# A decoder layer on one core: the end of the FFN in seven tiles of 128 tokens instead of eight of 112, and new tables of the order

## The chip, the cores and the metric

The kernel runs on one core of one Trainium2 chip. The metric is the device time of one execution in microseconds (us); smaller is better. In the profile the core's engines are called PE (TensorE, matmuls), PEld (its weight loads), DVE (VectorE), ACT (ScalarE), POOL (GpSimd) and SP (SyncE, which only issues transfers). Each engine works through its own queue in order and waits there for what its next instruction needs.

## What is computed

One layer of a decoder with post-norm, for 8 sequences of 112 tokens with 256 channels (896 tokens), all in float32:

```python
x = layernorm(x + self_attention(x))               # 16 heads of 64
x = layernorm(x + cross_attention(x, ctx, mask))   # 16 heads of 16, 375 keys
x = layernorm(x + ffn(x))

def ffn(x_):                                       # x_: (896, 256)
    idx = argmax(x_ @ router.T)                    # one of 8 experts a token
    y = down[idx] @ (silu(gate[idx] @ x_) * (up[idx] @ x_))        # hidden 512
    ys = (silu(x_ @ w_gate_s.T) * (x_ @ w_up_s.T)) @ w_down_s.T    # shared expert
    return y + ys

def layernorm(x):                                  # no scale, no shift of its own
    return (x - mean(x)) / sqrt(var(x) + 1e-5)
```

## The kernel before

**The order of the work** is written out by hand. Nine steps run one after another (lines 562 to 578 and 899). In step s three sequences are at work: the self-attention of sequence s, the cross-attention of sequence s-1, and what is left of sequence s-2. A step is a table of words (lines 28 to 50); `step` (line 532) reads the words from left to right and calls the piece of each, and since every engine's queue is in order, a table fixes how the pieces stand on every engine. `STEP` serves steps 1 to 5; `FIRST`, `STEP6`, `STEP7` and `LAST` serve steps 0, 6, 7 and 8. A `+` at a word has VectorE copy the piece's result out of the matmul memory (PSUM), a `-` has ScalarE do it.

The words of the steps:

- `k`, `u`, `c`: projections that are prepared ahead (queries and keys of the next pair of sequences, values, keys and values of the context). A product of them goes through the helper at line 248.
- `s`, `e`, `w`, `t`, `v`: scores, exponentials, weights, transposes and attention of self-attention (lines 329 to 379); `o`, `n`: its output projection and norm (381, 390); `q1`, `q2`: transposes and queries for the cross-attention (404, 408).
- `S`, `E`, `W`, `U`, `T`, `V`: the same of cross-attention (431 to 503), four heads at a time. `S` writes two score buffers, and the ring has two (line 86); `s` writes one.
- `F1` to `F4`: output projection, norm, transposes and router product of sequence s-2 (508 to 528); `f1` to `f4` are those of the last sequence.

**The FFN** is in `LAST`. `a0` to `a3` and `b0` to `b3` are the shared expert's gate and up products for the first half of the tokens (`shared_raw`, 607, of 448 = 4 x 112 tokens), `h0` to `h3` both products for the second half (`shared_half`, 615), `g0` and `g1` the silu of the first half (`silu_raw`, 627). `r` and `p` (`route_1`, 686) choose each token's expert; `R` and `P` (`route_2`, 700) count its place, `place_i`, and POOL scatters the tokens' rows to these places in DRAM (`to_places`, 661, one indirect DMA a sequence). `L` loads each expert's 128 rows (864), `A` transposes them, `B` makes the gate and up products, `C` the down product, which is stored to DRAM as `y_d` (796 to 831). A ninth, small tile takes up to 32 rows beyond an expert's 128; `x` (`beyond`, 739) works out whose they are. `C0` to `C4` also load the weights of experts 4 to 7 and of the small tile (880).

Then comes the end, once for each sequence b: `Y` gathers the 112 rows of the sequence from `y_d` by `place_i` (676), `D` adds the shared expert's down product, takes mean and variance and raises the variance to the power -0.5 on POOL (632, 224), and `Z` normalizes on VectorE and stores (643):

```python
def normalize(dst, src, mean, rs):
    V.tensor_scalar(dst, src, mean, rs, ALU.subtract, ALU.mult)
```

The store goes out on SP. A last branch (920) repeats part of this where more rows are left; with these inputs it isn't taken.

Of the kernel before, what the change touches and what calls it, by code (L numbers as in the profile page):

```python
# [25 lines left out]


STEP = """
S0 E0 k2 s0 u1- e0 T00+ F1 w0 c0 T02- S1 E1 u0- T01+ t00+ W0 s1 T10- T11- e1 c1 T12+ U0+ w1 V0 S2 c4
k3- t01- F2 F3 k0 t10+ t11- E2 v0+ v1- S3 T20+ E3 T22- o W1 T30- c2 n F4 T31+ k1- q1 U1- c3 T21+ q2  # L30
T32- V1
"""
STEP6 = """
S0 E0 c0 s0 c1 e0 T00+ T02- S1 c4 E1 w0 W0 T01- s1 u1- T10- T11- e1 u0+ U0- w1 t00- F1 T12- c3 t01-
S2 t10+ t11- V0 E2 v0+ v1- S3 T20- E3 F2 o n T21- W1 T30- c2 F3 T32- q1 F4 T22- T31- q2 U1+ V1
"""
STEP7 = """
S0 E0 c0 s0 c1 e0 S1 T00- E1 T01+ s1 c4 T02- T10- W0 U0- e1 w0 T12- w1 T11- S2 V0 t00+ t01- E2 F1
t10- v0- t11+ F2 S3 T20- v1+ E3 F3 o T30- n W1 T22- c3 T32- T21+ F4 q1 c2 T31- U1- q2 V1
"""  # L40
FIRST = """
k6 k4 u0- k5- k7+ s0 e0 s1 k3- u3- k1- e1 k2 u1- k0 w0 w1 t00+ t01+ u2- t10+ t11- v0+ v1+ z o c0 n
c1 c3 q1 c4 q2 c2
"""
LAST = """
S0 E0 F1 a2- S1 E1 a1- T00+ b0- T02+ F2 W0 T01- S2 T10+ T12- b1- E2 T11+ U0+ S3 V0 F3 E3 T20+ a3+
T22+ T21+ a0+ W1 T30- T31- F4 T32- U1- r V1 f1 R f2 b2+ f3 f4 b3- p P L0 h2 L1 h0 h1 A0 g1 A1 B0 L2
B1 A2 x C0 B2 A3 A4 C1 C2 B3 B4 A5 A6 C3 B5 C4 B6 A7 C5 B7 g0 A8 C6 B8 C7 C8 Y0 Y1 Y2 Y3 D0 Y4 Y5 D1
h3 Z0 Y6 D2 Z1 Y7 D3 Z2 D4 Z3 D5 Z4 D6 Z5 D7 Z6 Z7
"""  # L50


# [1 line left out]
def decoder_layer(  # L54
# [19 lines left out]
    E, _, H = upT.shape  # L74
    KH = H // P
    NTT = NT // P
    HB = B // 2
    HT = HB * S

    NG = 4  # L80
    NOV = (NT - 1) // P
# [2 lines left out]
    const = ctx.enter_context(tc.tile_pool(name="const", bufs=1))  # L84
# [4 lines left out]
    V, A, G = nc.vector, nc.scalar, nc.gpsimd  # L89
# [7 lines left out]
    def m_tile():  # L97
        return ps_m.tile([P, 512], F32, tag="mm", name="mm")
# [10 lines left out]
    ac = sa.enter_context(tc.tile_pool(name="ac", bufs=1))  # L109
# [5 lines left out]
    wo1 = ac.tile([P, NC, D], F32, name="wo1")  # L115
    bo1 = ac.tile([S, D], F32, name="bo1")
    xres = const.tile([S, B, D], F32, name="xres")
    r = const.tile([S, B, D], F32, name="r")
    mv = const.tile([S, B, 2], F32, name="mv")
    x2T = const.tile([P, KD, NT], F32, name="x2T")  # L120
    lgs = const.tile([S, B, E], F32, name="lgs")
    rt = const.tile([P, KD, E], F32, name="rt")
# [1 line left out]
    load = nc.sync.dma_start  # L124
# [77 lines left out]

    xs_d = tc.dram_tile([E * NT, D], F32, name="xs_d")
    y_d = tc.dram_tile([E * NT, D], F32, name="y_d")
    fill_sb = const.tile([P, D], F32, name="fill_sb")
    G.memset(fill_sb, 0.0)

    cap = xc.tile([S, S2], F32, name="cap")
# [9 lines left out]
    def stats(dst, src):  # L218
        st = small.tile([P, 6], F32, tag="st", name="st")
        n = src.shape[0]  # L220
        V.bn_stats(st[:n], src)
        V.bn_aggr(dst, st[:n])

    def rstd_of(var):

        n = var.shape[0]
        rs = small.tile([P, 1], F32, tag="rs", name="rs")
        V.tensor_scalar(rs[:n], var, EPS, None, ALU.add)  # L228
        G.tensor_tensor(rs[:n], rs[:n], mhalf[:n], ALU.pow)  # L229
        return rs[:n]  # L230

    def normalize(dst, src, mean, rs):
        V.tensor_scalar(dst, src, mean, rs, ALU.subtract, ALU.mult)
# [8 lines left out]
    def copy(on, dst, src):  # L242

        (V.tensor_copy if on == "+" else A.copy)(dst, src)  # L244

    def product(out_, pairs):
        for i, (lhsT, rhs) in enumerate(pairs):
            nc.tensor.matmul(out_, lhsT, rhs, start=(i == 0), stop=(i == len(pairs) - 1))  # L248
# [7 lines left out]
    def project(p, half):  # L256

        if half == 0:
            qk[p] = [ap_.tile([P, NC, 2 * S], F32, tag=n, name=n) for n in ("qT", "kT")]

        def piece(on, n, c):
            ps = m_tile()
            for i in range(2):
                product(
                    ps[:, bass.ts(i, 2 * S)],
                    [
                        (wqkv[n][:, k, bass.ts(c + i, P)], xT_sb[:, k, bass.ts(p, 2 * S)])
                        for k in range(KD)
                    ],
                )  # L270
# [52 lines left out]
    class SelfAttention:  # L323
# [57 lines left out]
        def project(self, on):  # L381
            b = self.b
            G.tensor_tensor(xres[:, b, :], xres[:, b, :], bo1, ALU.add)
            ps = m_tile()
            product(ps[:S, :D], [(self.aoT[:, c, :], wo1[:, c, :]) for c in range(NC)])
            V.tensor_tensor(r[:, b, :], ps[:S, :D], xres[:, b, :], ALU.add)
            stats(mv[:, b, :], r[:, b, :])
            self.rs = rstd_of(mv[:, b, 1:2])

        def norm(self, on):  # L390
            b = self.b
            normalize(xres[:, b, :], r[:, b, :], mv[:, b, 0:1], self.rs)


    class CrossAttention:
# [112 lines left out]
        def finish_1(self):  # L508
            b = self.b
            ps = m_tile()  # L510
            product(ps[:S, :D], [(self.xoT[:, k, :], wx["o"][:, k, :]) for k in range(KD)])
            V.tensor_tensor(r[:, b, :], ps[:S, :D], xres[:, b, :], ALU.add)
            stats(mv[:, b, :], r[:, b, :])
            self.rs = rstd_of(mv[:, b, 1:2])

        def finish_2(self):
            b = self.b
            normalize(xres[:, b, :], r[:, b, :], mv[:, b, 0:1], self.rs)

        def finish_3(self):  # L520
            transposed(x2T[:, :, bass.ts(self.b, S)], xres[:, self.b, :])
# [60 lines left out]
    fc = ctx.enter_context(tc.tile_pool(name="fc", bufs=1))  # L582
# [12 lines left out]
    swd = fc.tile([P, KH, D], F32, name="swd")  # L595
# [19 lines left out]
    def shared_half(hc):
        ug = sc_tile()
        for i, w in enumerate((swu, swg)):
            product(
                ug[:, i, :HT], [(w[:, k, bass.ts(hc, P)], x2T[:, k, HT:]) for k in range(KD)]
            )  # L620
        sg = fp.tile([P, 512], F32, tag="sg", name="sg", bufs=3)
        A.activation(sg[:, :HT], ug[:, 1, :HT], AF.Silu)
        V.tensor_tensor(hS1[:, hc, :], ug[:, 0, :HT], sg[:, :HT], ALU.mult)

    rstds = {}

# [2 lines left out]
        A.activation(raw["g"][:, h, :], raw["g"][:, h, :], AF.Silu)  # L629
        V.tensor_tensor(raw["u"][:, h, :], raw["u"][:, h, :], raw["g"][:, h, :], ALU.mult)  # L630

    def last_sum(b):

        h = raw["u"] if b < HB else hS1
        ps = m_tile()
        product(
            ps[:S, :D], [(h[:, hc, bass.ts(b % HB, S)], swd[:, hc, :]) for hc in range(KH)]
        )
        V.tensor_tensor(r[:, b, :], ps[:S, :D], r[:, b, :], ALU.add)
# [18 lines left out]
    place_i = small_tile("place_i", None, I32)  # L658
# [14 lines left out]
            tc.declare_no_dep(i.ins, other.ins, reason="distinct places")  # L673
        sent.append(i)

    def from_places(b):
        G.indirect_dma_start(  # L677
            out=r[:, b, :],
            out_offset=None,
            in_=y_d[:, :],  # L680
            in_offset=bass.IndirectOffsetOnAxis(ap=place_i[:, b : b + 1], axis=0),
            bounds_check=E * NT - 1,
            oob_is_err=False,
        )
# [293 lines left out]
```

## Time and profile before

| | |
|---|---|
| median of 4 runs | 417.94 us (417.71 to 418.68) |
| the profiled execution's own time | 417.9 us |
| its span, from the first to the last instruction | 416.1 us |
| mean granted TensorE clock | 0.995 of full speed |
| step 3, from S0 to S0 of step 4 | 139.4 to 177.6 us |
| LAST, from S0 | 300.65 us |
| A0, the first expert's transposes | 340.49 us |
| the last matmul of C8 | ends at 389.46 us |
| the last norm | ends at 410.46 us |

The profile is one execution. A page of it has the busy time of each engine; a timeline has one row for each stretch of equal instructions: start and duration in us, engine, line, operation, output<-inputs, shapes, the number of instructions, and in brackets the idle time ahead of them with what ended it. Matmuls are pipelined and their ends are modelled, so a block's cost on TensorE is read from its start to the next block's start. In the rows of line 248, `mm<-xT_sb,wq` is a `k` piece, `mm<-wv,xT_sb` a `u`, `mm<-cT,wxk` and `mm<-wxv,cT` a `c`; L437 is `S`, L336 is `s`, L485 is `T`, L365 is `t`, L372 is `v`, L496 is `V`, L474 is `U`, L239 the transposes in `q1`, `F3` and `f3`.

### The profile page before, as it was taken

Reading aid. Unit: us, or ns where it says so; the run is one execution under the profiler, and the core shown is the slowest. Engines: PE = TensorE matmul, PEld = TensorE weight load, DVE = VectorE, ACT = ScalarE, POOL = GpSimd, SP = SyncE. Lnnn points to the kernel's source line nnn. Section 1 sums busy time; section 2 is a strip of 40 time slices with the busy share of each in tenths; the row PEclk is TensorE's granted clock in tenths of the full one; section 3 lists DMA queues with packets and bytes.
Section 4 is the critical chain, followed back from the end, with each engine's and each line's share of the span. In section 5 each row is a group of like instructions: output and inputs, shape, how many; then the busy total and the mean of one; then the engine's idle time right before and its main releaser. Section 6 shows DMA issues by size and latency. Waiting matters only on the chain.

```text
span 416.1 us, 8496 instructions
## 1 busy us (share of the span) xinstructions
PE 398.7 (96%) x3347; PEld 310.8 (75%) x3347; DVE 239.9 (58%) x672; ACT 187.6 (45%) x476; POOL 75.2 (18%) x111
## 2 busy tenths in 40 slices
PE   5999999999999999999999999999999989999991
PEld 4977768867886887688678877867857559999661
DVE  0173685578458666855784587489487524223173
ACT  1232465456627554654566286577476221112000
POOL 3021112103012200221030112104100520000281
PEclk9999999999999999999999999999999999999998
DMA  8980398099010001000000100000694140895132
GB/s 271 308 229 0 100 372 277 12 372 351 11 39 2 2 1 38 2 2 16 23 2 2 38 0 2 2 2 2 217 373 170 45 137 11 287 375 178 40 110 61
DMA packets 38334, 46.61 MB, mean 112 GB/s; under 512 B 2181, under 2 KB 31378, under 8 KB 38290
## 3 DMA queue, kind: packets, MB, share of 16 engines
q1 hardware_dynamic: 36978, 43.66, 32.3%
q0 software_dynamic: 768, 1.84, 1.5%
q8 instruction: 28, 0.46, 0.4%
q10 hardware_dynamic: 544, 0.52, 0.4%
q14 instruction: 16, 0.13, 0.1%
HBM read 28.41 MB, written 17.60 MB: 111 GB/s over the span
## 4 chain that ended last, share of the span: by engine, by line
PE 87%; POOL 4%; issue 4%; DMA 3%; DVE 2%; ACT 0%; SPq 0%; POOLq 0%; DVEq 0%
PE mm L248 46%; PE pt L485 10%; PE sc L248 7%; PE sc L437 7%; PE mm L496 5%; PE sc L336 4%; PE mm L372 3%; PE pt L365 3%; POOL r L677 1%; POOL xs_d L664 1%; DMA wq<-in_w_qkv 1%; POOL rs L229 1%; PE pt L239 1%; DMA xs_d<-xres,place_i 1%; DMA xs<-xs_d 1%
## 5 line engine op out<-in xcount | busy, mean ns | idle before, releaser
L455 ACT ACTIVATE ex<-ex,nm 112x375 f32<-112x375 f32 x128 | 76.5, 599 | 47.4 <-DVE nm L451 46.7
L451 DVE CUSTOM_DVE_ANT_0 ex<-sc,cap 112x375 f32<-112x375 f32 x128 | 63.6, 544 | 10.0 <-PE sc L437 9.6
L485 PEld LDWEIGHTS pt<-ident,ex 112*125 112x125 f32 x384 | 50.9, 188 | 17.1 <-issue 10.0
L485 PE MATMUL pt<-ident,ex 112*125 112x112 f32 x384 | 55.1, 275 | 0.1
L244 ACT COPY exT<-pt 125x448 f32<-125x448 f32 x56 | 28.3, 527 | 29.2 <-PE pt L485 29.1
L358 POOL TENSOR_TENSOR pr<-pr,den 112x896 f32<-112x896 f32 x16 | 26.9, 1683 | 80.3 <-DVE den L357 43.6
L229 POOL TENSOR_TENSOR rs<-rs,mhalf 112x1 f32<-112x1 f32 x24 | 13.4, 559 | 144.6 <-DVE rs L228 144.5
L248 PE MATMUL mm<-xT_sb,wq 128*128 128x224 f32 x128 | 28.9, 373 | 5.0 <-DMA wq<-in_w_qkv 5.0
L248 PE MATMUL mm<-wv,xT_sb 128*112 128x512 f32 x64 | 31.1, 608 | 0.0
L248 PEld LDWEIGHTS mm<-xT_sb,wq 128*128 128x128 f32 x128 | 24.4, 199 | 8.5 <-DMA wq<-in_w_qkv 5.0
L437 PE MATMUL sc<-kc,qz 32*112 32x375 f32 x256 | 29.8, 519 | 0.1
L248 PE MATMUL mm<-wo,aoT 128*112 128x256 f32 x128 | 29.0, 380 | 0.0
L244 DVE COPY exT<-pt 125x448 f32<-125x448 f32 x40 | 24.8, 622 | 7.0 <-PE pt L485 6.5
L248 PE MATMUL mm<-xT_sb,wk 128*128 128x224 f32 x128 | 27.4, 359 | 0.0
L248 PE MATMUL mm<-wxv,cT 128*125 128x256 f32 x96 | 25.6, 389 | 0.0
L248 PEld LDWEIGHTS mm<-xT_sb,wk 128*128 128x128 f32 x128 | 24.4, 195 | 1.5 <-issue 0.5
L248 PEld LDWEIGHTS mm<-wo,aoT 128*112 128x112 f32 x128 | 22.0, 177 | 4.5 <-DVE aoT L244 0.2
L455 ACT ACTIVATION_READ_ACCUMULATOR ex<-ex,nm 112x1 f32 x128 | 23.9, 187 | 0.0
L248 PE MATMUL mm<-cT,wxk 128*128 128x375 f32 x64 | 23.2, 486 | 0.0
L244 DVE COPY prT<-pt 112x448 f32<-112x448 f32 x16 | 9.8, 620 | 20.7 <-PE pt L365 20.7
L496 PE MATMUL mm<-exT,vc 125*32 125x112 f32 x768 | 21.7, 261 | 0.0
L345 DVE TENSOR_REDUCE mx<-sc 112x8 f32<-112x896 f32 x16 | 17.4, 1087 | 5.9 <-PE sc L336 5.4
(156 smaller groups left out, 640.4 us busy)
## 6 DMA issues: line engine op xcount, KB each, us to landing
xs_d<-fill_sb SPq DMA_DIRECT2D x1, 7168.0 KB, 24.2
y_d<-fill_sb SPq DMA_DIRECT2D x1, 7168.0 KB, 24.9
wg<-in_gateT SPq DMA_DIRECT2D x9, 512.0 KB, 7.3
wu<-in_upT SPq DMA_DIRECT2D x9, 512.0 KB, 8.0
wd<-in_downT SPq DMA_DIRECT2D x9, 512.0 KB, 9.3
cT<-in_ctxT SPq DMA_DIRECT2D x8, 375.0 KB, 3.6
wv<-in_w_qkv SPq DMA_DIRECT2D x2, 512.0 KB, 7.7
wo<-in_w_out SPq DMA_DIRECT2D x1, 1024.0 KB, 13.9
```

The costliest lines, as they stand in the source:

```text
L229: G.tensor_tensor(rs[:n], rs[:n], mhalf[:n], ALU.pow)
L244: (V.tensor_copy if on == "+" else A.copy)(dst, src)
L248: nc.tensor.matmul(out_, lhsT, rhs, start=(i == 0), stop=(i == len(pairs) - 1))
L336: nc.tensor.matmul(sc[:S, j, bass.ts(c, S)], qT[rows, 4 * g + c, self.tok], kT[rows, 4 * g + c, self.tok], start=True, stop=True,)
L345: V.tensor_reduce(self.mx, scv, AX.X, ALU.max)
L358: G.tensor_tensor(pr, pr, den.unsqueeze(3).to_broadcast([S, 2, 4, S]), ALU.mult)
L365: nc.tensor.transpose(pt[:S, bass.ts(c, S)], self.pr[g][:, j, c, :], ident[:S, :S])
L437: nc.tensor.matmul(sc[i // 2][:S, i % 2, :S2], self.qz[rows, par, c, :], kc[rows, c, :], start=True, stop=True,)
L451: V.tensor_tensor_reduce(ex[:, i, :], self.sc[g][i // 2][:S, i % 2, :S2], cap, -1.0, BIG, ALU.add, ALU.min, nm[:, i : i + 1],)
L455: A.activation(ex[:, i, :], ex[:, i, :], AF.Exp, bias=nm[:, i : i + 1], scale=-1.0, accum_out=den[:, i, g % 2 : g % 2 + 1],)
L485: nc.tensor.transpose(pt[:JT, bass.ts(i, S)], self.ex[g][:, i, bass.ts(t, JT)], ident[:S, :S])
L496: nc.tensor.matmul(av[32 * i : 32 * i + 32, 0:S], vcs[self.b % 2][:, t, 4 * c + i, bass.ds(32 * par, 32)], self.exT[2 * c + par][:, t, bas ...
```

## The change

The end works on seven tiles of 128 tokens (7 x 128 = 896) instead of eight of 112. For this the first half of the shared expert's hidden values takes 512 tokens and the second 384; `r` and `mv` get 128 partitions; and the places, which lie as [112 tokens, 8 sequences], are laid anew as [128 tokens, 7 tiles]: `i0` writes them to DRAM and `i1` reads them back, both on SP. The last norm becomes two instructions: VectorE makes the shift -mean x rs, one number a token, and ScalarE applies scale and shift. `fill_sb` moves to another pool. All five tables are new.

```diff
 STEP = """
-S0 E0 k2 s0 u1- e0 T00+ F1 w0 c0 T02- S1 E1 u0- T01+ t00+ W0 s1 T10- T11- e1 c1 T12+ U0+ w1 V0 S2 c4
-k3- t01- F2 F3 k0 t10+ t11- E2 v0+ v1- S3 T20+ E3 T22- o W1 T30- c2 n F4 T31+ k1- q1 U1- c3 T21+ q2
-T32- V1
+S0 k2 E0 s0 u1- T00- e0 S1 w0 T02- c1 E1 k0 s1 W0 T01- t00- F1 u0- e1 T10+ w1 U0- c0 T12+ k3- t01+
+T11- c4 t10+ t11- S2 V0 E2 v0+ v1+ S3 F2 E3 T20+ T22+ o T30+ n W1 c3 F3 k1- T31- q1 F4 c2 T32+ T21-
+q2 U1- V1
 """
 STEP6 = """
-S0 E0 c0 s0 c1 e0 T00+ T02- S1 c4 E1 w0 W0 T01- s1 u1- T10- T11- e1 u0+ U0- w1 t00- F1 T12- c3 t01-
-S2 t10+ t11- V0 E2 v0+ v1- S3 T20- E3 F2 o n T21- W1 T30- c2 F3 T32- q1 F4 T22- T31- q2 U1+ V1
+S0 E0 c0 s0 c1 e0 T00+ T01- S1 c4 E1 T02- u1- w0 s1 T10- T12- e1 W0 w1 u0- T11- U0- S2 V0 t00+ t01-
+F1 t10- t11- E2 v0+ v1- F2 S3 E3 T20+ o T30- T31+ c2 n T22- F3 c3 q1 T21- W1 F4 T32- U1+ q2 V1
 """
 STEP7 = """
-S0 E0 c0 s0 c1 e0 S1 T00- E1 T01+ s1 c4 T02- T10- W0 U0- e1 w0 T12- w1 T11- S2 V0 t00+ t01- E2 F1
-t10- v0- t11+ F2 S3 T20- v1+ E3 F3 o T30- n W1 T22- c3 T32- T21+ F4 q1 c2 T31- U1- q2 V1
+S0 E0 c1 s0 c0 e0 S1 T00- E1 T01+ s1 c4 T10- T11- W0 U0- e1 w0 w1 T02- T12- S2 V0 t00+ t01- E2 F1
+t10- v0+ t11- S3 T20+ v1+ E3 T21+ F2 o T30- n c2 F3 T22- W1 c3 q1 T31- F4 T32- U1- q2 V1
 """
 FIRST = """
-k6 k4 u0- k5- k7+ s0 e0 s1 k3- u3- k1- e1 k2 u1- k0 w0 w1 t00+ t01+ u2- t10+ t11- v0+ v1+ z o c0 n
-c1 c3 q1 c4 q2 c2
+k6 k7- k4 k5- s0 e0 s1 u3+ u1- e1 w0 w1 c1 u0- k2 c2 u2- z t10- t11+ k0 t00- t01+ c4 v0+ v1+ o n c0
+k1+ q1 c3 q2 k3+
 """
 LAST = """
-S0 E0 F1 a2- S1 E1 a1- T00+ b0- T02+ F2 W0 T01- S2 T10+ T12- b1- E2 T11+ U0+ S3 V0 F3 E3 T20+ a3+
-T22+ T21+ a0+ W1 T30- T31- F4 T32- U1- r V1 f1 R f2 b2+ f3 f4 b3- p P L0 h2 L1 h0 h1 A0 g1 A1 B0 L2
-B1 A2 x C0 B2 A3 A4 C1 C2 B3 B4 A5 A6 C3 B5 C4 B6 A7 C5 B7 g0 A8 C6 B8 C7 C8 Y0 Y1 Y2 Y3 D0 Y4 Y5 D1
-h3 Z0 Y6 D2 Z1 Y7 D3 Z2 D4 Z3 D5 Z4 D6 Z5 D7 Z6 Z7
+S0 E0 a1+ a2- T00- S1 E1 T02- T01+ b0- S2 F1 T10+ W0 T12- E2 b1- T11+ U0+ F2 a0+ T20- T21- S3 E3 V0
+T22+ F3 a3+ T30- W1 T31- r F4 T32- U1- V1 f1 R f2 b2+ f3 f4 p h2 P L0 h1 b3- x h0 A0 L1 A1 L2 i0 B0
+g0 B1 A2 C0 B2 A3 C1 B3 C2 A4 A5 C3 B4 B5 i1 A6 C4 A7 B6 C5 A8 B7 C6 g1 B8 C7 C8 Y0 Y1 Y2 Y3 h3 D0
+D1 Z0 Y4 Y5 D2 Y6 D3 Z1 D4 Z2 D5 Z3 Z4 D6 Z5 Z6
 """
...
-    HB = B // 2
-    HT = HB * S
+    FT = 4
+    HT, HT2 = FT * P, NT - FT * P
...
-    r = const.tile([S, B, D], F32, name="r")
-    mv = const.tile([S, B, 2], F32, name="mv")
+    r = const.tile([P, B, D], F32, name="r")
+    mv = const.tile([P, B, 2], F32, name="mv")
...
-    fill_sb = const.tile([P, D], F32, name="fill_sb")
+    place_d = tc.dram_tile([NT, 1], I32, name="place_d")
+    fill_sb = ac.tile([P, D], F32, name="fill_sb")
...
-    def last_sum(b):
-
-        h = raw["u"] if b < HB else hS1
+    def last_sum(i):
+        h, n = (raw["u"], i) if i < FT else (hS1, i - FT)
         ps = m_tile()
-        product(
-            ps[:S, :D], [(h[:, hc, bass.ts(b % HB, S)], swd[:, hc, :]) for hc in range(KH)]
-        )
-        V.tensor_tensor(r[:, b, :], ps[:S, :D], r[:, b, :], ALU.add)
-        stats(mv[:, b, :], r[:, b, :])
-        rstds[b] = rstd_of(mv[:, b, 1:2])
+        product(ps[:, :D], [(h[:, hc, bass.ts(n, P)], swd[:, hc, :]) for hc in range(KH)])
+        V.tensor_tensor(r[:, i, :], ps[:, :D], r[:, i, :], ALU.add)
+        stats(mv[:, i, :], r[:, i, :])
+        rstds[i] = rstd_of(mv[:, i, 1:2])
 
-    def last_norm(b):
-        normalize(r[:, b, :], r[:, b, :], mv[:, b, 0:1], rstds[b])
-        load(out=out[bass.ts(b, S), :], in_=r[:, b, :])
+    def last_norm(i):
+        shift = mv[:, i, 0:1]
+        V.tensor_scalar(shift, shift, rstds[i], -1.0, ALU.mult, ALU.mult)
+        A.activation(r[:, i, :], r[:, i, :], AF.Identity, bias=shift, scale=rstds[i])
+        load(out=out[bass.ts(i, P), :], in_=r[:, i, :])
...
+    place_2 = fc.tile([P, NTT], I32, name="place_2")
+
+    def places_out():
+        load(out=place_d[:, :].rearrange("(b s) o -> s (b o)", s=S), in_=place_i)
+
+    def places_in():
+        load(out=place_2, in_=place_d[:, :].rearrange("(i p) o -> p (i o)", p=P))
...
-            out=r[:, b, :],
+            out=r[:, i, :],
...
-            in_offset=bass.IndirectOffsetOnAxis(ap=place_i[:, b : b + 1], axis=0),
+            in_offset=bass.IndirectOffsetOnAxis(ap=place_2[:, i : i + 1], axis=0),
```

Where the second half's products and the uses of `r` and `mv` in the attentions name sizes, they follow (`HT2` columns, `r[:S, ...]`).

## The prediction

> **What bounds the kernel now.** I read the page first, then the chain that ended last in order of time, then the timeline of each stage. The page says that TensorE is the bound nearly throughout:
>
> ```profile
> span 416.1 us, 8496 instructions
> ...
> PE 398.7 (96%) x3347; PEld 310.8 (75%) x3347; DVE 239.9 (58%) x672; ACT 187.6 (45%) x476; POOL 75.2 (18%) x111
> ```
>
> The profiled execution took 417.9 us, the span and 1.8 us around it; the median of four is 417.94, so the sum is made against 417.9. A difference of 0.2%, 0.84 us, is about what a measurement of this kernel can tell from none.
>
> I split the span in three. In steps 1 to 5 a period lasts 38.2 us, and the TensorE timeline shows each block of matmuls starting when the one before is through:
>
> ```profile
> 143.28 1.69 PE L248 MATMUL mm<-xT_sb,wq 128*128 128x224 f32 x8
> 144.81 0.93 PE L365 MATMUL pt<-ident,pr 112*112 112x112 f32 x8
> ...
> 160.57 0.90 PE L437 MATMUL sc<-kc,qz 32*112 32x375 f32 x8
> 161.40 1.78 PE L248 MATMUL mm<-xT_sb,wq 128*128 128x224 f32 x8
> 163.11 1.04 PE L336 MATMUL sc<-kT,qT 64*112 64x112 f32 x16
> ```
>
> No row carries an idle time, so a new order can't take waits out here. But start to start the same projection costs 1.53 us among full blocks and 1.71 between two score blocks (L437, L336), which use a part of the array's rows. So a join from full to part rows, or back, costs about 0.1.
>
> The second stage is the way to the experts. It is a chain on POOL (eight scatters 1.245 apart), then a landing, then a load; TensorE fills it and still waits:
>
> ```profile
> 327.01 1.18 POOL L664 DMA_INDIRECT xs_d<-xres,place_i  x1 [0.59 <-DVE xres L233]
> ...
> 335.98 0.94 POOL L664 DMA_INDIRECT xs_d<-xres,place_i  x1 [0.31 <-issue]
> ...
> 338.52 3.67 SPq L866 DMA_DIRECT2D xs<-xs_d  x8
> ...
> 340.49 0.44 PE L800 MATMUL pt<-ident,xs 128*128 128x128 f32 x2 [0.72 <-DMA xs<-xs_d]
> ```
>
> The third is the end, where TensorE is no longer the bound:
>
> ```profile
> 392.27 1.02 POOL L677 DMA_INDIRECT r<-y_d,place_i  x1 [55.35 <-DMA y_d<-y]
> ...
> 395.09 0.42 DVE L639 TENSOR_TENSOR r<-mm,r 112x256 f32<-112x256 f32 x1 [5.18 <-DMA r<-y_d,place_i]
> ...
> 402.95 1.04 POOL L677 DMA_INDIRECT r<-y_d,place_i  x1 [0.18 <-issue]
> ...
> 408.01 0.42 DVE L639 TENSOR_TENSOR r<-mm,r 112x256 f32<-112x256 f32 x1
> ...
> 409.44 0.58 POOL L229 TENSOR_TENSOR rs<-rs,mhalf 112x1 f32<-112x1 f32 x1 [0.94 <-DVE rs L228]
> 410.05 0.41 DVE L233 TENSOR_SCALAR r<-r,mv,rs 112x256 f32<-112x256 f32 x1 [0.44 <-POOL rs L229]
> ```
>
> The eighth gather is issued at 402.95, 2.8 us suffice for it (392.27 to 395.09), but its sum starts at 408.01: the last four tiles go at VectorE's pace, one per 1.53 to 1.77 us (403.19, 404.96, 406.48, 408.01), of which 0.41 is the norm.
>
> **Steps 1 to 5: -0.5.** The pieces of a step are the same, only their order is new. I counted joins in both orders. Before there are eleven: S0-k2, k2-s0, s0-u1, T02-S1, S1-u0, t00-s1, s1-T10, U0-V0, S2-c4, S3-T20, T32-V1. After there are ten: S0-k2, k2-s0, s0-u1, T00-S1, S1-T02, k0-s1, s1-T01, t11-S2, S3-T20, U1-V1 (S2-V0 and V0-v0 cost none; the rows of S after V1 show none either). That is 0.1 less in each of five steps. Could the new order wait? I walked it with the old durations; the tightest places are S1's second half, which needs the buffer that e0's subtraction frees (free at S0 + 5.8 us, needed at 6.15), T20, whose fourth exponential is done about 4.4 us after S2 starts and is needed at 4.9, and S0, which needs q2's evacuation (1.05 us) and comes 1.5 after it. None waits, with 0.3 us in hand. The lower bound of this term is -1.0 (two joins); the upper is that the margin of 0.3 is wrong by as much again in every step, +1.5.
>
> **FIRST, STEP6, STEP7: -0.5.** FIRST holds the same pieces; k7 moves up to 14.8 us, where its weights, issued at 2.85 with 7.1 to landing, are there; u3 and u1 need weights that landed at 12.7. I take nothing. In STEP6 the second transposes (L239) come at 265.88 and wait for the norm, ready 2.8 us after the projection o ended (263.09); the four transposes ahead of them last 0.86 start to start where 0.42 is usual, so 0.44 is lost. After, T30, T31, c2, T22, F3 and c3 (3.2 us) stand between, and the wait is covered. One join less gives 0.1. Bounds: 0 to -0.6. STEP7 keeps its wait at S1 (1.83 us instead of 0.83) in both orders: 0.
>
> **The first half's raw products: +1.2.** a0 to a3 and b0, b1, which stand before R, now stream 512 columns instead of 448. A block of 448 lasts 1.52 start to start, one of 512 (wv in FIRST) 1.72: six times 0.20. This stretch runs without a wait up to R at 324.3, so all of it is on the path. The second half's products get 64 columns cheaper (3.01 to 2.57 each, by the 375-column row's 0.315 a matmul), but three of the four only fill the POOL chain, whose length from R to A0 (324.3 to 340.5) nothing changes. So A0 comes as late after R as before, and TensorE's wait there grows from about 0.9 to some 2 us; it is not counted twice. The granted clock stays 1.00 until 412 though TensorE idles from 407.4, and is 0.50 only in 412 to 416, so a wait of 2 us should not lower it. The Trainium skill (TensorE: Matmul & The Clock Gate, What's actually happening) speaks of half the clock after an idle window of about 3.4 us: were the wait to reach that, an estimate by it is 1.7 us more for the next window; by the trace's row it is nothing.
>
> **Experts: 0.** The same matmuls, contiguous from A1 to C8 in the trace. x moves ahead of A0; before, its VectorE instructions (350.17 to 353.49) held C0's sum back, and the loads behind it. g1 (1.09 on VectorE) moves between C6 and B8; C7's 1.73 on TensorE hides it from h's product, which C8 needs; without that cover it costs up to 1.1. A8 moves from after B7 to before it and needs the small tile's rows at 378.25 instead of 381.92; they are issued at 375.76 and land 1.7 later: 0.8 in hand.
>
> **The two place copies: 0.** Each moves 896 words of 4 bytes as 896 packets, which no row shows. i0 goes out behind the xs loads, at about 342, and has 25 us. i1 stands on SP behind expert 7's loads (out by 367.2, since C3 now precedes B4, which lasts 3.57) and ahead of C4's store (373.4) and the small tile's rows. Below: 1.5 us to landing (the 32 KB store of y). Above: 9.3 (bq, 128 packets under full queues). By the mean packet (36978 packets, 32.3% of 16 engines x 416.1 us: 58 ns) it is 896 x 58 / 16 = 3.3 us and a landing; I take 5. It is free up to 9.4 (367.2 + 9.4 + 1.7 = 378.3), so all but the top costs nothing. r and mv with 128 rows and fill_sb in another pool add no instruction. The Trainium skill (DMA: Bandwidth & Descriptors, Rules for kernel authors) speaks against it: a non-contiguous last dimension makes one descriptor per element. By that page's 10.5 ns a packet, taken as one stream, an estimate is 9.4 us for i1, the very edge; the trace's rows say less.
>
> **The end: -2.8.** With C8 where it was, gathers again go out at 392.27, 393.60, 394.90, 396.19. On TensorE h3 (2.57) now precedes D0 and D1, which end near 395.4, in time for the first landing; each later sum costs 1.77. POOL: the powers of D0 and D1 at 397.2 and 397.8, then Y4 at 398.6, Y5 at 399.95, the power of D2, Y6 at 401.7, which is usable at 404.5. VectorE per tile: add 0.46, statistics 0.46, 0.22, variance 0.2, and 0.15 for the shift instead of 0.41: D2 at 398.05, D3 at 399.4, D4 at 401.4 (its gather), D5 at 402.9, D6 at 404.65; its power at 406.0, its shift at 406.6, ScalarE's Identity from 406.8. For that the nearest rows are 0.37 (copy, 128x256) and 0.57 (Identity with a bias, 128x375); I take 0.45. The norm ends at 407.2 instead of 410.46: -3.3. A gather of 128 rows instead of 112 costs POOL between 1.0 (no change) and 1.16 (by rows); seven of them give -2.3. I take the middle, -2.8. The store and the 3.7 us after it stay. A table load (1.28) for Identity is not in the built order; it would be hidden before the first shift.
>
> **Sum.** -0.5 - 0.5 + 1.2 - 2.8 = -2.6: 415.3. All low ends: -1.0 - 0.6 + 1.0 - 3.3 = -3.9, 414.0; all high: +1.5 + 0 + 1.3 - 2.3 = +0.5, 418.4.
>
> **Rivals.** (1) The new tables wait: 0.3 in each steady step and STEP6's wait not saved, 415.3 + 1.5 + 0.4 = 417.2. For it: margins of 0.3; against it: they come from rows. (2) The end does not do what the change says, because gathers and sums bind it instead of VectorE: only the last tile's 1.5 is won, 416.6. Against it: Y6 is usable before VectorE is free. (3) Slower: i1's packets hold the queue ahead of the small tile's rows, and A8 waits with all of TensorE's work behind it. It costs from a landing of 9.4 us on, one for one, cancels the gain at 12 and makes the kernel slower by 0.2% from 12.8; at 15 us the time is 420.9. For it: 128 packets took 8.3 and 9.3 us at the start; against it: there the DMA engines were full, here they have emptied.
>
> **Chances.** Forecast 0.64, (1) 0.16 at 417.2, half of it within 0.2%; (2) 0.11 at 416.6, a quarter within; (3) 0.09. Faster 0.64 + 0.08 + 0.08 = 0.80, same 0.11, slower 0.09. The range from 414.0 to 417.4 takes in the forecast's low end and (1) and (2), and leaves (3) and the worst sums out.
>
> **What would show it.** Right: a period of 38.1 with no idle rows; R later by about 0.2 against before and A0 as much; a wait of 2 us before A0; i1 landing within 9 us and no wait at A8; counted from C8's last matmul, the last add about 15.2 us later (18.5 before) and the last norm's end 17.8 (21). Wrong: long L437 or L485 blocks in the steady steps, a wait ahead of A8, gathers over 1.1 us, or sums that start at gather landings to the end.

## The result and the profile after

| | before | after |
|---|---|---|
| median of the runs | 418.18 us (67 runs, 417.30 to 419.45) | 417.61 us (44 runs, 416.40 to 419.27) |
| ratio, 95% interval | | 0.9988 (0.9982 to 0.9993) |
| the profiled execution | 417.9 us, span 416.1 | 417.08 us, span 415.3 |

The change made the kernel about 0.6 us faster, 0.12%; the forecast was 2.6. The interval leaves out 1, but 0.12% is less than the 0.2% from which the prediction speaks of a difference.

The profile cuts the span at the same places in both kernels. (In the table ahead of the change, 139.4 and 177.6 are starts of S2; S0 of steps 3 and 4 are at 122.36 and 160.57. The period, 38.2, is the same.) The end of C8 is taken at the start of the block behind it, 389.39 in before.

| stretch | before | after | difference | forecast |
|---|---|---|---|---|
| start to S0 of step 1 | 47.38 | 47.72 | +0.34 | 0 |
| S0 of step 1 to S0 of step 6 | 189.61 | 189.47 | -0.14 | -0.5 |
| STEP6 | 32.74 | 32.37 | -0.37 | -0.5 with STEP7 |
| STEP7 | 30.92 | 31.04 | +0.12 | |
| LAST: S0 to R | 23.65 | 25.01 | +1.36 | +1.2 |
| R to A0 | 16.19 | 16.28 | +0.09 | 0 |
| A0 to the end of C8's matmuls | 48.90 | 48.84 | -0.06 | 0 |
| from there to the end of the last norm | 21.07 | 18.91 | -2.16 | -2.8 |
| to the end of the span | 5.64 | 5.66 | +0.02 | 0 |

The page of after:

```profile
span 415.3 us, 8472 instructions
...
PE 397.3 (96%) x3339; PEld 310.0 (75%) x3339; DVE 238.6 (57%) x668; ACT 190.3 (46%) x482; POOL 73.6 (18%) x109
```

A steady step of after, TensorE's timeline (its lines are one higher than before's):

```profile
160.82 0.90 PE L438 MATMUL sc<-kc,qz 32*112 32x375 f32 x8
161.65 1.78 PE L249 MATMUL mm<-xT_sb,wq 128*128 128x224 f32 x8
...
166.14 0.59 PE L486 MATMUL pt<-ident,ex 112*125 112x112 f32 x4
166.66 1.04 PE L438 MATMUL sc<-kc,qz 32*112 32x375 f32 x8
167.63 0.69 PE L486 MATMUL pt<-ident,ex 112*125 112x112 f32 x4
```

The block at 166.66 is S1. It lasts 0.97 to the next start where S0, the same eight matmuls, lasts 0.83, in each of steps 1 to 5. Its second half takes the score buffer that e0 frees, and e0's subtraction is in VectorE's queue at

```profile
165.58 1.09 DVE L351 TENSOR_TENSOR pr<-sc,mx 112x896 f32<-112x896 f32 x1
```

which ends at 166.67, when S1 starts. No row shows an idle time: the wait lies inside the block, and only its length tells it. The way to the experts, from the timelines of POOL, SP and TensorE:

```profile
328.32 1.19 POOL L666 DMA_INDIRECT xs_d<-xres,place_i  x1 [0.59 <-DVE xres L234]
...
337.29 0.94 POOL L666 DMA_INDIRECT xs_d<-xres,place_i  x1 [0.30 <-issue]
...
339.83 3.67 SPq L877 DMA_DIRECT2D xs<-xs_d  x8
...
341.89 0.44 PE L811 MATMUL pt<-ident,xs 128*128 128x128 f32 x2 [2.29 <-DMA xs<-xs_d]
```

Everything comes 1.3 later than before, and TensorE waits 2.29 instead of 0.72 before the first transposes. And the end:

```profile
393.78 1.04 POOL L688 DMA_INDIRECT r<-y_d,place  x1 [55.55 <-issue]
...
396.73 0.42 DVE L639 TENSOR_TENSOR r<-mm,r 128x256 f32<-128x256 f32 x1 [2.03 <-DMA r<-y_d,place]
...
400.10 1.06 POOL L688 DMA_INDIRECT r<-y_d,place  x1 [0.18 <-issue]
...
404.01 0.42 DVE L639 TENSOR_TENSOR r<-mm,r 128x256 f32<-128x256 f32 x1 [1.64 <-DMA r<-y_d,place]
...
406.78 0.41 DVE L639 TENSOR_TENSOR r<-mm,r 128x256 f32<-128x256 f32 x1
...
408.80 0.21 DVE L645 TENSOR_SCALAR mv<-mv,rs 128x1 f32<-128x1 f32 x1 [0.54 <-POOL rs L230]
409.04 0.60 ACT L646 ACTIVATE r<-r,mv,rs 128x256 f32<-128x256 f32 x1 [0.15 <-DVE mv L645]
```

There are seven sums instead of eight, but the fifth waits 1.64 us for a gather issued at 400.10, and the last norm ends 2.86 after the last sum's start (2.45 in before).

So TensorE's products ahead of R and the end behaved about as forecast in kind. The questions for the chip: does A0 really hang on POOL; what do the tables, the norm and the gathers cost; and why do the medians show less (-0.6) than the profiles (-0.8, and -1.1 once a chance difference at the start, shown below, is taken out)?

### The profile page after: what moved, and what is told of

Its sections match the earlier page's. It is cut to its first block, busy times and chain, and to the rows that moved or that the text cites. A ratio compares the mean times of both kernels' runs of the same rounds, so it can differ in the third digit from the quotient of the medians.

```text
span 415.3 us, 8472 instructions
## 1 busy us (share of the span) xinstructions
PE 397.3 (96%) x3339; PEld 310.0 (75%) x3339; DVE 238.6 (57%) x668; ACT 190.3 (46%) x482; POOL 73.6 (18%) x109
## 4 chain that ended last, share of the span: by engine, by line
PE 87%; DMA 3%; issue 3%; POOL 3%; DVE 1%; ACT 0%; SPq 0%; POOLq 0%; DVEq 0%
PE mm L249 47%; PE pt L486 11%; PE sc L249 7%; PE sc L438 7%; PE mm L497 5%; PE sc L337 4%; PE mm L373 3%; PE pt L366 3%; POOL xs_d L666 1%; DMA wq<-in_w_qkv 1%; DMA r<-y_d,place 1%; POOL r L688 1%; PE pt L240 1%; POOL rs L230 1%; DMA xs_d<-xres,place_i 1%
## 5 line engine op out<-in xcount | busy, mean ns | idle before, releaser
L486 PE MATMUL pt<-ident,ex 112*125 112x112 f32 x384 | 56.1, 277 | 0.1
L230 POOL TENSOR_TENSOR rs<-rs,mhalf 112x1 f32<-112x1 f32 (+1 forms) x23 | 12.7, 552 | 113.5 <-DVE rs L229 112.1
L832 DVE TENSOR_TENSOR hT<-sc,sg 128x512 f32<-128x512 f32 x8 | 5.5, 692 | 30.4 <-ACT sg L830 30.4
L497 PEld LDWEIGHTS mm<-exT,vc 125*32 125x32 f32 x768 | 17.9, 110 | 5.4 <-issue 3.8
```

Of the source, the lines that this page charges most:

```text
L486: nc.tensor.transpose(pt[:JT, bass.ts(i, S)], self.ex[g][:, i, bass.ts(t, JT)], ident[:S, :S])
L497: nc.tensor.matmul(av[32 * i : 32 * i + 32, 0:S], vcs[self.b % 2][:, t, 4 * c + i, bass.ds(32 * par, 32)], self.exT[2 * c + par][:, t, bas ...
```

## The experiments

All are edits of the kernel after. A ratio is to the kernel before, measured beside it; after's is 0.9988.

### e1: the first half three tiles instead of four

```diff
-    FT = 4
+    FT = 3
```

> The kernel after (417.6 us) with its first half 3 tiles (384 columns) instead of 4. Theory T (the end won 2.3 us, but the six raw products ahead of R pay 1.3 of it back, since R to A0 is a chain on POOL of fixed length, in which TensorE waits 2.45 us): a block of 384 columns takes 1.30 start to start instead of 1.73, so R comes 6 x 0.43 = 2.6 us earlier; the three halves h0 to h2 get 3 x 0.87 = 2.6 dearer and fill TensorE's wait at A0, whose length falls to under 0.3; h3 gets 0.87 dearer ahead of the end's sums. 417.6 - 2.6 + 0.87 = 415.9 (415.0 to 416.6). Rival X (the new step tables cost what the end won) and rival Y (the norm on ScalarE and the wait at the fifth gather cost it): TensorE has the same columns to stream in all, so 417.6 (417.2 to 418.0).

Measured: 415.47 us, ratio 0.9924 (0.9905 to 0.9944). S0 to R takes 23.21 instead of 25.01, A0 comes without a wait of note, 16.22 after R. TensorE's row at A0, with no idle time printed ahead of it:

```profile
340.38 0.44 PE L811 MATMUL pt<-ident,xs 128*128 128x128 f32 x2
```

T holds, though two of its terms are off and nearly cancel. S0 to R fell by 1.80, not 2.6, since two of the six products cover something: behind a2, T00 now takes 0.89 to the next block instead of 0.52; behind a3 the next experiment shows what. And h3's 0.87 isn't paid at the end: from C8 to the last norm it is 18.70 instead of 18.91.

### e2: a3 behind R

```diff
-T22+ F3 a3+ T30- W1 T31- r F4 T32- U1- V1 f1 R f2 b2+ f3 f4 p h2 P L0 h1 b3- x h0 A0 L1 A1 L2 i0 B0
+T22+ F3 T30- W1 T31- r F4 T32- U1- V1 f1 R f2 b2+ f3 f4 p h2 P L0 h1 b3- a3+ x h0 A0 L1 A1 L2 i0 B0
```

> The kernel after with one raw product of the first half, a3, put into TensorE's wait ahead of A0 instead of ahead of R. T: R comes 1.75 earlier and with it the chain on POOL and A0; the wait at A0 falls from 2.45 to about 0.7; 417.6 - 1.75 = 415.9 (415.4 to 416.4). X and Y: 417.6 (417.2 to 418.0). If the chain to A0 isn't set by POOL but by what stands behind R on SP or VectorE, the gain is lost there: 417.0 to 417.6.

Measured: 417.98 us, 0.9990 (0.9976 to 1.0004): nothing won, the expectation of T missed. TensorE's timeline of e2 tells why:

```profile
321.51 1.13 PE L486 MATMUL pt<-ident,ex 112*125 112x112 f32 x8 [1.35 <-ACT x2T L241]
```

Without a3 the next transposes wait 1.35 us for ScalarE, which is at the exponentials until then: a3 had been their cover. R comes only 0.12 earlier against S0 of LAST (24.89 instead of 25.01), and TensorE, now with a3 behind R, reaches A0 without a wait, 16.50 after R. So this run doesn't speak against T, but "all of it is on the path" holds for the added columns (1.36 where 1.2 was forecast), not for a whole product.

### e3: before's step tables

FIRST, STEP, STEP6 and STEP7 as before the change, LAST and the end as after.

> The kernel after with the four tables FIRST, STEP, STEP6 and STEP7 of before; LAST, the seven tiles and the norm as in after. T, by the stages of the two profiles: the five steps +0.1, STEP6 +0.37, STEP7 -0.12, the start 0 to -0.3: 417.8 (417.5 to 418.2). X (the new tables cost what the end won, so that the old ones give it back): 415.5 to 416.5. Y: as T.

Measured: 417.92 us, 0.9991 (0.9979 to 1.0003). Its profile has the old lengths, 38.21 a step, 32.74 for STEP6, 30.91 for STEP7: the new tables win 0.35, and X falls. But its experts, the same instructions as in after, take 48.62 from A0 to the start of C8's last block instead of 46.99. The granted clock (last but two) in the same two stretches, first after, then e3; the rows give the stretch, its length, and the busy time of PE, PEld, DVE, ACT and POOL with the number of instructions:

```profile
344.00:346.00 2.00, 2.00 (x20) 2.00 (x19) 0.00 (x0) 0.00 (x0) 0.00 (x0) 1.00 0.69 113
346.00:348.00 2.00, 2.00 (x20) 2.00 (x19) 0.69 (x1) 1.33 (x2) 0.00 (x0) 1.00 0.00 0
```

```profile
344.00:346.00 2.00, 2.00 (x11) 2.00 (x11) 0.00 (x0) 0.00 (x0) 0.00 (x0) 0.50 0.63 129
346.00:348.00 2.00, 2.00 (x15) 2.00 (x15) 0.00 (x0) 0.00 (x0) 0.00 (x0) 0.72 0.06 4
```

From 343.7 to 347.1 TensorE was granted half its clock, and it did 11 matmuls in 2 us instead of 20. That is the first sign of the missing piece; e12 to e14 take it up.

### e4: the last norm on VectorE

```diff
-        V.tensor_scalar(shift, shift, rstds[i], -1.0, ALU.mult, ALU.mult)
-        A.activation(r[:, i, :], r[:, i, :], AF.Identity, bias=shift, scale=rstds[i])
+        normalize(r[:, i, :], r[:, i, :], shift, rstds[i])
```

> The kernel after with the last norm in one VectorE instruction (0.41) as before, instead of a shift (0.21) and ScalarE's Identity (0.60). T: for the last tile the power's end to the norm's end falls from 0.83 to about 0.5; the four norms ahead of the last sum cost VectorE 0.2 more each, 0.8 in all, if VectorE has no idle time there, which it has (1.64 at the fifth sum); together 0 to +0.6: 417.6 to 418.2. Rival Y (the norm on ScalarE costs what the end won): 416.0 to 416.8.

Measured: 417.14 us, 0.9976 (0.9960 to 0.9993), an interval that meets after's. In the profile the stretch from C8's end to the norm's end is 18.16 instead of 18.91. The last norm:

```profile
408.31 0.58 POOL L230 TENSOR_TENSOR rs<-rs,mhalf 128x1 f32<-128x1 f32 x1 [1.26 <-DVE rs L229]
408.93 0.41 DVE L234 TENSOR_SCALAR r<-r,mv,rs 128x256 f32<-128x256 f32 x1 [0.44 <-POOL rs L230]
```

0.41 follows the power, where after has the shift, a hand-over and 0.60. Rival Y is right in kind, with half of its size: scale and shift on ScalarE cost 0.4 at the last tile; the rest is a gather that landed sooner (the fifth sum waits 0.45).

### e5: all gathers first

```diff
-g0 B1 A2 C0 B2 A3 C1 B3 C2 A4 A5 C3 B4 B5 i1 A6 C4 A7 B6 C5 A8 B7 C6 g1 B8 C7 C8 Y0 Y1 Y2 Y3 h3 D0
-D1 Z0 Y4 Y5 D2 Y6 D3 Z1 D4 Z2 D5 Z3 Z4 D6 Z5 Z6
+g0 B1 A2 C0 B2 A3 C1 B3 C2 A4 A5 C3 B4 B5 i1 A6 C4 A7 B6 C5 A8 B7 C6 g1 B8 C7 C8 Y0 Y1 Y2 Y3 Y4 Y5
+Y6 h3 D0 D1 D2 D3 D4 Z0 Z1 D5 Z2 Z3 Z4 D6 Z5 Z6
```

> The kernel after with all seven gathers issued ahead of the first power on POOL, and the first shifts put behind the fifth sum. In after the fifth sum waits 1.64 us for its gather, issued at 400.10 behind two powers, and TensorE's last product waits 0.51 for the buffer that this sum frees. Theory G (the late gather sets the end): the fifth gather goes out 0.9 earlier, the sum's wait goes, the last sum comes when the last product ends, 0.5 to 0.8 earlier: 417.6 - 0.6 = 417.0 (416.7 to 417.3). Rival (the end runs at the pace of the products and VectorE, the gather's wait is only in their slack): 417.6 (417.3 to 418.0).

Measured: 417.50 us, 0.9986 (0.9975 to 0.9998). In the profile the fifth sum's wait for its gather is gone (0.43 for a product is left), and the last sum comes 15.41 after C8's matmuls instead of 16.05, as G expects. The median can't tell 0.6 from nothing here; the profile speaks for G.

### e6: T02 ahead of S1

```diff
-S0 k2 E0 s0 u1- T00- e0 S1 w0 T02- c1 E1 k0 s1 W0 T01- t00- F1 u0- e1 T10+ w1 U0- c0 T12+ k3- t01+
+S0 k2 E0 s0 u1- T00- e0 T02- S1 w0 c1 E1 k0 s1 W0 T01- t00- F1 u0- e1 T10+ w1 U0- c0 T12+ k3- t01+
```

> The kernel after with the transposes T02 put ahead of S1's second score block in STEP instead of behind w0, 0.43 us that stand between e0 and S1. Theory S (the order won its joins, and S1, 0.97 instead of 0.83, pays them back by waiting for e0's subtraction): the wait of 0.14 goes in each of five steps, 417.6 - 0.6 = 417.0 (416.8 to 417.3). Rival (the joins are dearer elsewhere and S1's wait is the score block's own variation): 417.6 (417.3 to 417.9).

Measured: 416.51 us, 0.9969 (0.9953 to 0.9986). TensorE's timeline of e6:

```profile
165.06 1.02 PE L486 MATMUL pt<-ident,ex 112*125 112x112 f32 x8
166.01 0.90 PE L438 MATMUL sc<-kc,qz 32*112 32x375 f32 x8
166.84 1.53 PE L249 MATMUL mm<-cT,wxk 128*128 128x375 f32 x4
```

S1 is 0.83 long and the period 38.05 instead of 38.19, in each step. S is shown: the new order had won its join and lost it to e0. The five steps win 0.7 in the profile; the time fell by 1.1, below S's range, and the profile doesn't show why.

### e7: one scatter ahead of the last finish

`route_2` gets a third argument, the number of scatters that it issues itself; G issues the others.

```diff
-T22+ F3 a3+ T30- W1 T31- r F4 T32- U1- V1 f1 R f2 b2+ f3 f4 p h2 P L0 h1 b3- x h0 A0 L1 A1 L2 i0 B0
+T22+ F3 a3+ T30- W1 T31- r F4 T32- U1- V1 R f1 G f2 b2+ f3 f4 p h2 P L0 h1 b3- x h0 A0 L1 A1 L2 i0 B0
...
-    raw_pieces["R"] = lambda on: route_2(0, B - 2)
+    raw_pieces["R"] = lambda on: route_2(0, B - 2, 1)
+    raw_pieces["G"] = lambda on: [to_places(b) for b in range(1, B - 2)]
```

> The kernel after with R's places worked out, and the first of its six scatters issued, ahead of the last finish's sum and power, the other five behind them; TensorE's pieces stay otherwise. Theory P (A0 is set by POOL's chain from the first scatter on, and TensorE's 2.45 us at A0 are slack): the second to the eighth scatter come 1.2 to 1.8 earlier and with them A0 and all behind it: 417.6 - 1.5 = 416.1 (415.7 to 416.6). Rival (TensorE's products or the loads behind the last scatter set A0): 417.6 (417.2 to 418.0). If the power, now behind one scatter, makes the last norm and with it the last two scatters later by more than the chain won: 417.6 to 418.5.

Measured: 415.89 us, 0.9943 (0.9924 to 0.9962). POOL and TensorE in e7:

```profile
325.66 1.19 POOL L666 DMA_INDIRECT xs_d<-xres,place_i  x1 [3.41 <-DVE place_i L728]
327.16 0.57 POOL L230 TENSOR_TENSOR rs<-rs,mhalf 112x1 f32<-112x1 f32 x1 [0.30 <-DVE rs L229]
327.93 1.10 POOL L666 DMA_INDIRECT xs_d<-xres,place_i  x1 [0.20 <-issue]
...
340.31 0.82 PE L812 MATMUL pt<-ident,xs 128*128 128x128 f32 x4 [0.70 <-DMA xs<-xs_d]
```

TensorE's pieces are the same; the chain on POOL starts sooner, and A0 comes 1.1 earlier against S0 of LAST than in after (40.18 instead of 41.29), the wait falls to 0.70. P holds. The time fell by 1.7, more than the profile's 1.1: the difference is again what the experiments below explain.

### e8: e1 and e4 together

> The first half of 384 columns (2.1 us faster than after) and the last norm on VectorE (0.5 faster) together. If both are right and stand in different stretches, they add: 417.6 - 2.1 - 0.5 = 415.0 (414.6 to 415.4). If the norm's gain came from the fifth sum's idle time alone, and the longer h3 shifts the sums, only the first stays: 415.5.

Measured: 414.45 us, 0.9909 (0.9889 to 0.9930). In the time the parts add, and 0.5 more, just below the range; in this profile they don't quite, since its fifth sum waits for a gather (0.86).

### e9, e10, e11: towards a faster kernel

e9 has e4's norm and the end as `Y0 Y1 Y2 Y3 Y4 h3 D0 D1 Y5 Y6 D2 Z0 D3 Z1 D4 Z2 D5 Z3 Z4 D6 Z5 Z6`. e10 is e9, e6 and e7 together. e11 is e10 and:

```diff
 STEP6 = """
-S0 E0 c0 s0 c1 e0 T00+ T01- S1 c4 E1 T02- u1- w0 s1 T10- T12- e1 W0 w1 u0- T11- U0- S2 V0 t00+ t01-
+S0 E0 c0 s0 c1 e0 T00+ T01- T02- S1 c4 E1 u1- w0 s1 T10- T12- e1 W0 w1 u0- T11- U0- S2 V0 t00+ t01-
...
 STEP7 = """
-S0 E0 c1 s0 c0 e0 S1 T00- E1 T01+ s1 c4 T10- T11- W0 U0- e1 w0 w1 T02- T12- S2 V0 t00+ t01- E2 F1
+S0 E0 c1 s0 c0 e0 c4 S1 T00- E1 T01+ s1 T10- T11- W0 U0- e1 w0 w1 T02- T12- S2 V0 t00+ t01- E2 F1
```

> The kernel after with its end alone changed: the norm on VectorE, five gathers ahead of the first power and two behind the second, the norms put between the later sums. Theory E (once gathers and norm are out of the way the end is TensorE's: h3 2.68 and seven sums of 1.77 back to back behind C8): the last add starts 15.1 behind h3's start instead of 16.05, and the norm ends 2.46 behind it instead of 2.86: 417.6 - 1.35 = 416.25 (415.9 to 416.7). Rival (gathers still set the sums, so only the norm's 0.7 is won): 416.9 (416.7 to 417.3).

> The kernel after with the end of e9, T02 ahead of S1 in STEP (e6) and one scatter ahead of the last finish (e7); first half of 512 columns as in after. The three stand in three stretches and add: 417.6 - 1.35 - 0.7 - 1.7 = 413.9 (413.4 to 414.6). If the earlier A0 only moves a wait to the expert loads, 415.0 to 415.6.

> As e10, and in STEP6 the transposes T02, in STEP7 the projection c4 put ahead of S1, whose second block waits for e0's subtraction (0.97 and 1.83 instead of 0.83). Theory S (the wait is TensorE running ahead of e0): 0.14 and 1.0 go, 413.9 - 1.1 = 412.8 (412.3 to 413.6). Rival (c4 is then missing behind S1, where it covers E1's exponentials, and the wait moves there): 413.9 (413.5 to 414.3).

Measured: e9 417.39 us, 0.9973 (0.9962 to 0.9984), 0.1 above the rival's range. Its last sum starts 15.8 behind h3's start, not 15.1, but gathers aren't what sets it (the fifth sum waits 0.11): VectorE, now with the norms in its queue, reaches it 0.37 after TensorE's last product, and TensorE itself has only two buffers, so its third product starts at 397.08, when the first sum has taken the first landing.

e10 took 414.45 us, 0.9905 (0.9890 to 0.9920): in the range, the fastest version with e8, and faster than both kernels. The sum behind its forecast is right only in total, since the end won 0.65 in the profile and not 1.35.

e11 took 415.93 us, 0.9928 (0.9915 to 0.9942), slower than e10: what the rival says happened, and more of it. In STEP6 a transpose now waits 0.53 for its buffer; in STEP7 S1 is 0.92 instead of 1.83, but transposes behind it wait 0.29, 0.23 and 0.28. In e11's profile the granted clock then fell to 0.50, from 281.5 to 284.9, and STEP7 lasted 33.04 instead of 31.03.

### e12: no place copies

```diff
     def places_out():
-        load(out=place_d[:, :].rearrange("(b s) o -> s (b o)", s=S), in_=place_i)
+        pass
...
     def places_in():
-        load(out=place_2, in_=place_d[:, :].rearrange("(i p) o -> p (i o)", p=P))
+        pass
...
+    G.iota(place_2, pattern=[[P, NTT]], base=0, channel_multiplier=1)
```

> The kernel after without the two copies of the places, 896 packets of 4 bytes each: GpSimd writes the row numbers 0 to 895 into the tile at the start, so the gathers fetch rows in their natural order, and that part of the computation is left out. Theory T (the copies are hidden behind the experts): 417.6 (417.2 to 417.9). Rival (they hold the queue ahead of C4's store and the small tile's rows, or the engines during the loads): 416.6 to 417.1.

Measured: 417.57 us, 0.9971 (0.9960 to 0.9982; 7 runs). The median is T's and the ratio is between the two; outside the experts no stretch behind A0 differs from after's by more than 0.2 in the profile. The copies are hidden, up to 0.2 or so. They landed after 7.6 and 8.9 us in after. And the granted clock fell here too, to 0.50 from 342.9 to 346.3, with 48.62 for the experts as in e3.

### e13 and e14: is it the wait?

e13 puts a product of 512 columns that nothing reads between h0 and A0; e14 puts h0 behind B0.

```diff
-T22+ F3 a3+ T30- W1 T31- r F4 T32- U1- V1 f1 R f2 b2+ f3 f4 p h2 P L0 h1 b3- x h0 A0 L1 A1 L2 i0 B0
+T22+ F3 a3+ T30- W1 T31- r F4 T32- U1- V1 f1 R f2 b2+ f3 f4 p h2 P L0 h1 b3- x h0 X A0 L1 A1 L2 i0 B0
...
+    def unread():
+        ps = m_tile()
+        product(ps[:, :HT], [(swu[:, k, 0:P], x2T[:, k, 0:HT]) for k in range(KD)])
+
+    raw_pieces["X"] = lambda on: unread()
```

```diff
-T22+ F3 a3+ T30- W1 T31- r F4 T32- U1- V1 f1 R f2 b2+ f3 f4 p h2 P L0 h1 b3- x h0 A0 L1 A1 L2 i0 B0
-g0 B1 A2 C0 B2 A3 C1 B3 C2 A4 A5 C3 B4 B5 i1 A6 C4 A7 B6 C5 A8 B7 C6 g1 B8 C7 C8 Y0 Y1 Y2 Y3 h3 D0
+T22+ F3 a3+ T30- W1 T31- r F4 T32- U1- V1 f1 R f2 b2+ f3 f4 p h2 P L0 h1 b3- x A0 L1 A1 L2 i0 B0
+h0 g0 B1 A2 C0 B2 A3 C1 B3 C2 A4 A5 C3 B4 B5 i1 A6 C4 A7 B6 C5 A8 B7 C6 g1 B8 C7 C8 Y0 Y1 Y2 Y3 h3 D0
```

> The kernel after with one product more in TensorE's wait ahead of A0: 512 columns (1.73 us) into a buffer that nothing reads. A0 stays where POOL's chain puts it. Theory C (the wait of 2.3 and A0's transposes, 3.2 us without a product, let the granted clock fall to 0.50 for 3.4 us in some executions, as in the profiles of e3 and e12, where the experts took 1.6 longer): the clock stays 1.00, the experts take 47.0 in every execution; with 2 falls in 7 profiles that is 0.5 less in the mean: 417.1 (416.8 to 417.4), and the times above 418 become rare. Rival (the wait is harmless, those two profiles are chance): 417.6, or more by what the product delays A0.

> The kernel after with h0 (2.57 us) put behind B0 instead of ahead of A0, so that TensorE's wait at A0 grows from 2.3 to about 4.9 and, with the transposes, 5.8 us pass without a product. The work moved behind the wait costs 2.57 in any case. Theory C: the clock falls in every execution, 1.6 us: 417.6 + 2.57 + 1.6 x 5/7 = 421.3 (420.8 to 421.8), the granted clock 0.50 for 3.4 us behind A0 and the experts 1.6 longer than their own 2.57. Rival (the wait doesn't matter for the clock): 420.2 (419.9 to 420.5), granted clock 1.00.

Measured: e13 417.03 us (416.33 to 417.98), 0.9968 (0.9957 to 0.9979): TensorE does 1.73 us more work, and the kernel is 0.6 us faster than after. Its experts take 46.98. e14 421.43 us, 1.0078 (1.0060 to 1.0095). TensorE's first transposes at A0 in e13, then in e14, and the clock's row in e14:

```profile
341.47 1.02 PE L811 MATMUL pt<-ident,xs 128*128 128x128 f32 x4 [0.67 <-DMA xs<-xs_d]
```

```profile
341.59 1.24 PE L811 MATMUL pt<-ident,xs 128*128 128x128 f32 x4 [5.02 <-DMA xs<-xs_d]
```

```profile
344.00:346.00 2.00, 2.00 (x11) 2.00 (x11) 0.00 (x0) 0.00 (x0) 0.00 (x0) 0.50 0.50 70
```

In e14 the clock was 0.50 from 339.9 to 346.7, twice as long as C says, with the first 1.7 us still in the wait; the experts took 2.0 longer than h0's own 2.68. Both times lie in C's ranges and outside the rival's.

The wait at A0 costs more than itself. In 2 of the 7 profiles that have it (after, e3, e4, e5, e6, e9, e12; 2.1 to 2.4 us long) the clock fell behind it, in e14's longer one it fell, and in the profiles with a wait of at most 0.72 it didn't fall there.

The record also has the mean granted clock of every execution, and 3.41 us at half the clock take 0.004 off that mean. After's 46 executions fall into two groups with nothing between them: 26 at 0.992 to 0.994, like its profile, with a median of 417.24 us, and 20 at 0.988 to 0.990, with 418.27. So the clock fell in about 20 of 46, which is 0.45 us in the mean, about what the medians lack against the profiles (-0.6 against -1.1). All six executions of e14 are at 0.986 or 0.987, and none of e1, e7, e8, e10 or e13 is under 0.991. The groups differ by 1.03 us and not by the 1.63 of the experts; why is not shown. e2 is an exception: 5 of its 12 executions are at 0.989 or 0.990 without a wait at A0. Its profile has no fall; the 1.35 us ahead of eight transposes may be the place.

Like compared with like, the executions of 0.992 and more have medians of 416.91 in e4, 416.89 in e5 and 416.09 in e6 against after's 417.24. They are few (8, 5 and 8), but the gains of the three profiles show in them.

## Why the prediction missed

**The step that failed is the price of the wait at A0.** The prediction had the wait itself right (about 2 us; 2.3) and A0 fixed to R (16.19 and 16.28; in all profiles 16.0 to 16.5). It then said "a wait of 2 us should not lower it", from the clock's rows at the end of before, where the clock stayed at 1.00 for 4.6 us of idle. One execution can't show what happens in a part of them. What the runs showed in its place is a fall to 0.50 for 3.4 us behind the wait in about 20 of 46 executions, 1.63 us in the experts of e3 and e12, and about 0.45 in the mean.

Why only in a part of them can be read from the traces. In all sixteen profiles the clock is granted in full for a whole number of stretches of 3.413 us before it changes (334.51 us, 98 of them, up to the fall in e3 and in e12; 273.07, 80, in e11; 331.09, 97, in e14), counted from the first grant, which itself comes at another moment in each execution. In e3 and e12 one such stretch held nearly the whole wait: TensorE was busy in 1.58 and 1.79 us of it, and the clock fell at its end. In after a boundary cut the wait in two (1.98 and 2.30 busy), and the clock stayed. It is a close thing: in e6 a stretch with 1.81 busy left the clock alone. This agrees with the Trainium skill (TensorE: Matmul & The Clock Gate, What's actually happening), which says that the window is free-running and about 3.4 us long. The prediction's estimate by that page for one fall was 1.7 us, and 1.63 was measured.

Where the page and the runs differ is the idle: it asks for a whole idle window, while in e3 and e12 a window that was busy for about half was enough. The same page (Part 4: PE-mode transpose) says that transposes don't count as busy in the same way. The runs agree: e11's fall came at the end of a stretch that was busy for 2.71 us, all but 0.06 of it transposes (and 4.0 us, from 277.5 to 281.5, held nothing but transposes and waits), while e6's 1.81, with 0.96 of products, didn't lower the clock. How much a transpose counts isn't measured.

**Steps 1 to 5, -0.5: -0.1.** "None waits, with 0.3 us in hand" was wrong for S1, by 0.14 in each step; e6 takes it away. The bound of +1.5 held it.

**FIRST, STEP6, STEP7, -0.5: -0.2.** FIRST is 0, as said: from the end of the kernel's second block to S0 of step 1 it is 37.16 before and 37.19 or 37.20 in every profile with the new table. STEP6 won 0.37 of 0.54, STEP7 lost 0.12. The +0.34 at the start is that second block: the full clock was first granted at 9.24 us in before's profile and at 9.94 in after's, and among the profiles with the new table it lies anywhere from 8.4 to 10.8, which is chance.

**The raw products, +1.2: +1.36.** Right, and e1 and e7 show that it could have been had back: what the second half saved went into the wait.

**The copies and the experts, 0: 0.** Right in the sum. i1 took 8.9 and not 5 us to land, 0.5 inside the bound of 9.4 from which A8 would have waited.

**The end, -2.8: -2.2.** Two sizes: Identity with scale and shift lasts 0.60, not 0.45 (the row with the same operands did not exist, and the copy's 0.37 pulled the value down), and the gathers were taken to be usable 2.8 after issue, while the fifth took 3.9. e4 puts the first at 0.4, e5 the second at 0.6; they overlap, and e9 shows a third limit behind them, TensorE's two buffers. From the fifth gather's issue to its sum it was 3.9 us in after and e7, 3.6 in e6 and 2.95 in e4. Why stays open; the first store of 128 KB goes out beside it in all of them.

The sum by these: -0.1 - 0.2 + 1.36 - 2.2 + 0.05 = -1.1 in the profile, and about 0.5 for the clock in the mean. So nearly 1.5 of the missing 2.0 us are terms of the right kind with the wrong size (the end 0.6, the steps 0.4, the other tables and the raw products 0.2 each), and 0.5 is the term put at nothing: the executions without a fall have a median of 417.24, still in the stated range. Of the rivals, the second (gathers bind the end, 416.6) described a part of what happened; the first named the tables' wait, with twice its size (0.3 a step); none had the clock.

## What to carry to other kernels

Work that is shaved off a stretch whose end another engine sets turns into a wait, and a wait of the matmul engine can cost a second time through its clock, in a part of the executions only; so fill it with work that stands on the path elsewhere (e1), or start the other engine's chain sooner (e7). Before a product is moved, ask what it covers (without a3's 1.73 us, R came 0.12 earlier). A wait inside a block carries no idle row: compare the block's length with its twin's.

## What the runs showed of the hardware

A product of 1.73 us that nothing reads made the kernel 0.6 us faster (e13).

The second block of the kernel, the same eight matmuls in all profiles, took 1.63 to 2.78 us, start to start. The rows of the profile print a granted clock of 1.00 there, but the trace's record of the clock only begins with the first full grant, at 8.4 to 10.8 us, 3.4 to 5.7 us behind the first matmul. At that moment the step from one matmul to the next goes from 0.37 to 0.19 us, inside this block. This alone moves a run's time by up to 1.1 us, and two single profiles can't be compared to better than that without cutting it out. The Trainium skill (TensorE: Matmul & The Clock Gate, What's actually happening) gives ±0.5 us for the transition point; these sixteen profiles spread over 2.3.

After the first grant, every change of the clock in the sixteen profiles came a whole number of stretches of 3.413 us later (80, 97, 98, 117 or 118 of them to the first fall).

A copy of 896 words of 4 bytes each landed after 7.6 us (out) and 8.9 us (in).
